# A macaron layer with routed feed-forwards: the rows of the experts' results are gathered tile by tile, and the sums are split alike

## The chip, the core and the metric

The kernel runs on one NeuronCore of a Trainium2 chip. TensorE (PE) multiplies matrices and writes PSUM; VectorE (DVE), ScalarE (ACT) and GpSimd (POOL) work on tiles of 128 partitions in SBUF (VectorE and ScalarE also on PSUM); SyncE (SP) starts most of the transfers. Each engine runs its own list of instructions in order and waits for others at semaphores. Transfers whose addresses come from a tile of indices (gathers) are started by POOL, in POOL's own order, and POOL is occupied while it prepares one.

The metric is the time of one execution on the device, in microseconds. The median of several executions without the profiler is compared; the profile is one more execution, recorded by the hardware.

## The reference

The input is four sequences of 256 tokens with 256 features. The layer is a half feed-forward, an attention, and another half feed-forward with the same weights:

```python
x = x + 0.5 * ffn(layernorm(x), router, w_in, w_out, bias)
x = x + attention(layernorm(x), w_q, w_k, w_v, w_o, b_o)
x = x + 0.5 * ffn(layernorm(x), router, w_in, w_out, bias)

def ffn(x, ...):                      # for each token
    logits = x @ router.T             # 8 experts
    top_vals, top_idx = top_k(logits, 2)
    gates = softmax(top_vals)
    # for each expert e: a, b = split(x @ w_in[e].T); o = (silu(a) * b) @ w_out[e].T
    return sum over the token's two experts of gate * o + bias
```

The hidden width of an expert is 512. The attention has 16 heads of 16 features, is causal, and divides the scores by the square root of 256.

## The kernel before

**Halves and experts.** The 1,024 tokens are worked as two halves, a and b, of four tiles of 128 tokens (two sequences of two tiles). The first feed-forward of the halves is called fa and fb, the second ga and gb. For each of them the tokens are routed (`route_half`): each token gets, for each of its two experts, a place in a table `o_d` in DRAM (`placei`, two indices for each token), and two gates `g`. Then `ffn_half` goes through the eight experts. The rows of an expert's tokens are gathered from DRAM into a tile `xg` (`fetched_rows`, a gather on POOL, three buffers), transposed on TensorE into `pxg` and copied by VectorE to `xT`. `inner(e)` makes four steps, f = 0 to 3, of a product `ph` (L727), the activation on ScalarE (L501) and two steps on VectorE (L502, L503), whose last result is called `hT`. "Step 1.2" below is expert 1, f = 2. `outer(e)` multiplies by `w_out` (L749) and sends the result to `o_d` (L512).

**The sums.** When a feed-forward is done, `combine` brings the results back to the tokens. It takes two tiles (a sequence) at a time. POOL adds half the bias to each tile (L526) and gathers for each token the rows of its first and second expert from `o_d` into tiles `oj` (L532, four buffers): four gathers for a sequence. Then VectorE adds gate times row to the tile (L542), four operations for a sequence. `combine` is a generator that yields after the gathers and after the sums of each sequence, so two yields for a sequence.

**What goes beside what.** The feed-forward of one half runs beside the attention of the other: fb with the attention of half a, ga with that of half b. `ffn_half` and `attention` are generators too, and the main part decides by calls of `run(generator, n)` how many steps of one are written between steps of the other. The first `LEAD` = 7 steps of the feed-forward come before the attention. The attention of a half begins in `ready()`, which makes the sums of a sequence and normalizes it; it is called for the first sequence at the start and for the second while the scores of the first are made. `project` transposes the normalized rows, has them copied by ScalarE (L311), and makes q, k and v (L809, L833), with ScalarE copying q and k out (L818, L822). `maxima` makes the scores (L862, L871, L880) and their maxima on VectorE (L888), head by head; `contexts` makes the weights and applies them; `finish` normalizes and projects. POOL adds the output bias to a tile (L846) behind the projection.

**What sets the order.** The order in which the program writes its instructions is only a start: a scheduler lays them out on each engine by when it expects their operands. `tc.issue_after(ins)` keeps what is written under it behind `ins` on the same engine. `m.hidden` is the last VectorE step of the feed-forward (L503) written so far, `m.gathered` the last gather of rows for an expert. So before the change the sums on VectorE are kept behind the last feed-forward step written, and the bias additions behind the last gather of `xg`. The gathers into `oj` are not held by anything but their operands: the table in DRAM, the indices, and a free buffer.

Of the kernel before, what the change touches and what calls it, by code (L numbers as in the profile page):

```python
# [12 lines left out]
I32 = mybir.dt.int32  # L13
# [3 lines left out]
ALU = mybir.AluOpType  # L17
AX = mybir.AxisListType

P = 128  # L20
# [5 lines left out]
def kernel(  # L26
# [25 lines left out]
    nc = tc.nc  # L52
# [10 lines left out]
    TPB = S // P  # L63
# [15 lines left out]
    LEAD = 7  # L79
# [19 lines left out]
    m = Pools()  # L99
# [11 lines left out]
    def run(steps, n=None):  # L111
        for _ in range(n) if n is not None else iter(int, 1):
            if next(steps, steps) is steps:
                return

    def bank(shape, name, tag="one", bufs=4):
        return ps.tile(shape, F32, tag=tag, name=name, bufs=bufs)
# [13 lines left out]
    for t in range(NTILE):  # L131
        xt = m.xs.tile([P, D], F32, tag="xa", name=f"x_{t}")
# [151 lines left out]
    def norm(xt, name, to=None):  # L284

        n = len(xt)
        mv = m.small.tile([P, n, 2], F32, tag="mv", name=f"mv_{name}")
        for t in range(n):
            st = m.small.tile([P, 6], F32, tag="st", name=f"st_{name}_{t}")
            nc.vector.bn_stats(st, xt[t])  # L290
            nc.vector.bn_aggr(mv[:, t, :], st)
        rstd = rsqrt(mv[:, :, 1], n, name, to)
        res = []
        for t in range(n):
            if t % TPB == 0:
                xn = m.wk.tile([P, TPB, D], F32, tag="xn", name=f"xn_{name}_{t}")
                res.append(xn)
            m.normed = nc.vector.tensor_scalar(
                xn[:, t % TPB, :], xt[t], mv[:, t, 0:1], rstd[:, t : t + 1], ALU.subtract, ALU.mult
            )  # L300
        return res

    def across(xt, name):

        n = len(xt)
        xT = m.wk.tile([P, NDC, n * P], F32, tag="xnT", name=f"xnT_{name}")
        for c in range(NDC):
            pt = bank([P, n * P], f"pxn_{name}_{c}")
            for t in range(n):
                nc.tensor.transpose(pt[:, ts(t, P)], xt[t][:, ts(c, P)], ident)  # L310
            nc.scalar.copy(xT[:, c, :], pt)  # L311
        return xT
# [201 lines left out]
    def combine(xt, o_d, placei, g, name, wide=False):  # L514

        for b in range(len(xt) // TPB):
            rows = []
            if wide and b == 1:  # L520
                two = [
                    m.wk.tile([P, 2, D], F32, tag="xn", name=f"oj_{name}_{t}") for t in range(TPB)
                ]
            for t in range(b * TPB, (b + 1) * TPB):
                with tc.issue_after(m.gathered.ins):
                    nc.gpsimd.tensor_tensor(xt[t], xt[t], bias_bc, ALU.add)  # L526
                for j in range(2):
                    if wide and b == 1:
                        oj = two[t % TPB][:, j, :]
                    else:  # L530
                        oj = m.wk.tile([P, D], F32, tag="oj", name=f"oj_{name}_{t}_{j}", bufs=4)
                    nc.gpsimd.indirect_dma_start(  # L532
                        out=oj,
                        out_offset=None,
                        in_=o_d,
                        in_offset=bass.IndirectOffsetOnAxis(ap=placei[:, t, j : j + 1], axis=0),
                    )
                    rows.append((t, j, oj))
            yield
            with tc.issue_after(m.hidden.ins):  # L540
                for t, j, oj in rows:
                    nc.vector.scalar_tensor_tensor(  # L542
                        xt[t], oj, g[:, t, j : j + 1], xt[t], ALU.mult, ALU.add
                    )
            yield


    def early_logits(xt, name):
# [251 lines left out]
    def project(xt, xn, b):  # L800

        xnT = across([xn[:, t, :] for t in range(TPB)], f"a{b}")
        qkT = []
        for i, wp in enumerate(wqk_sb):
            dst = m.wk.tile([P, NG, S], F32, tag=("qT", "kT")[i], name=f"qk_{b}_{i}")
            pq = bank([P, NDC, S], f"pq_{b}_{i}")
            for j in range(NDC):
                for c in range(NDC):
                    nc.tensor.matmul(  # L809
                        pq[:, j, :],  # L810
                        lhsT=wp[:, c, ts(j, P)],
                        rhs=xnT[:, c, :],
                        start=(c == 0),
                        stop=(c == NDC - 1),
                    )
            for p in range(2):
                if i == 0:
                    nc.scalar.activation(  # L818
                        dst[:, p::2, :], pq, AF.Copy, scale=own_scaled[:, p : p + 1]
                    )  # L820
                else:
                    nc.scalar.activation(  # L822
                        dst[:, p::2, :],
                        pq,
                        AF.Identity,
                        bias=first_row[:, p : p + 1],
                        scale=own[:, p : p + 1],
                    )
            qkT.append(dst)
        pv = bank([P, TPB, D], f"pv_{b}")  # L830
        for t in range(TPB):
            for c in range(NDC):
                m.step = nc.tensor.matmul(  # L833
                    pv[:, t, :],
                    lhsT=xnT[:, c, ts(t, P)],
                    rhs=wv_sb[:, c, :],
                    start=(c == 0),
                    stop=(c == NDC - 1),
                )
        v = v_pad[b % 2]  # L840
        for t in range(TPB):
            nc.scalar.copy(
                v[:, t, 0 : H * HV].rearrange("p (h d) -> p h d", d=HV)[:, :, 0:HD], pv[:, t, :].rearrange("p (h d) -> p h d", d=HD)
            )
        for t in range(TPB):
            nc.gpsimd.tensor_tensor(xt[t], xt[t], bo_bc, ALU.add)  # L846
        return *qkT, v
# [173 lines left out]
    def attention(x1, b0, x2, sums, behind):  # L1021

        n = len(x1) // TPB
        xn = []

        def ready():

            i = len(xn)
            if i < n:
                run(sums, 2)
                xn.extend(norm(x1[i * TPB : (i + 1) * TPB], f"a{b0 + i}"))

        ready()
        yield 4
        last = None
        for i in range(n + 1):
            b = b0 + i  # L1040
            scores = iter(())
            if i < n:
                xt = x1[i * TPB : (i + 1) * TPB]
                qT, kT, v = project(xt, xn[i], b)
                yield 1
                scores = maxima(qT, kT, b)
            if last is None:
                for g, _ in enumerate(scores):
                    if g == 1:
                        ready()  # L1050
                    yield 1
            else:
                ctxT = m.wk.tile([P, NG, S], F32, tag="ctxT", name=f"ctxT_{b - 1}", bufs=1)
                for g, _ in enumerate(contexts(*last[0], ctxT)):
                    more = next(scores, 0) is None
                    if g == 1:
                        ready()
                    yield 2 if more and g % 2 == 0 else 1
                for k, _ in enumerate(finish(ctxT, last[1], b - 1, x2)):
                    yield 1 if i < n else 1 - k  # L1060
                if i < n:
                    run(behind, 1)
            last = (qT, kT, v, b), xt
# [139 lines left out]
    ffn = ffn_half(fa, o_d["fa"], "fa")  # L1203
# [4 lines left out]
    with tc.issue_after(m.sourced.ins):  # L1208


        placei = const.tile([P, 1], I32, name="in_quadi")
# [19 lines left out]
    run(ffn)  # L1231
    ffn = ffn_half(fb, o_d["fb"], "fb")
    sums = combine(xa, o_d["fa"], *fa[2:4], "fa")
    run(sums, 1)
    run(ffn, LEAD)
    ya = []
    route = route_half(ya, 2, "ga", ga)
    run(beside(attention(xa, 0, ya, sums, route), ffn))
# [1 line left out]
    run(ffn)  # L1240
    ffn = ffn_half(ga, o_d["ga"], "ga")
    sums = combine(xb, o_d["fb"], *fb[2:4], "fb")
    run(sums, 1)
    run(ffn, LEAD)
    yb = []
    route = route_half(yb, 3, "gb", gb, True)
    run(beside(attention(xb, BPH, yb, sums, route), ffn))
# [2 lines left out]
    ysum = [bank([P, TPB, D], f"ysum_{i}") for i in range(BPH)]  # L1250
    ffn = ffn_half(gb, o_d["gb"], "gb", gb[5], ysum)
    sums = combine(ya, o_d["ga"], *ga[2:4], "ga")
    run(sums, 1)
    for b in range(BPH):
        run(ffn, LEAD)
        run(sums, 1)
        store(ya[b * TPB : (b + 1) * TPB], b * TPB)
        run(sums, 1)

    run(ffn, 5 * LATE[0] + 5 - BPH * LEAD)  # L1260
    sums = combine(yb, o_d["gb"], *gb[2:4], "gb", True)
    run(sums, 1)
    run(ffn, 9)
    run(sums)
    run(ffn)
    for t in range(TPH):
# [9 lines left out]
    n = nc.values_load(  # L1276
        topi[0:1, 0:1],
        min_val=0,
        max_val=HALF,
        skip_runtime_bounds_check_because="a count of at most the tokens of a half",  # L1280
    )
# [71 lines left out]
```

## Time and profile before

| | us |
|---|---|
| median of 3 runs | 407.78 |
| lowest and highest | 404.29, 407.96 |
| the profiled execution | 427.48 |
| its span, first to last instruction | 425.7 |

In the profiled execution TensorE is busy for 389.7 us, VectorE for 220.3, POOL for 117.3 and ScalarE for 105.2. The mean clock granted to TensorE is 0.956 of full speed. There are 8 gathers into `oj` for each of fa, fb, ga and gb, and 10 into `xg` for each (9 in fa). The chain of work that ended last is empty on this page, so the order of time on the engines has to be read instead.

In a line of the timeline the first number is the start from the beginning of the span, the second the length, both in us; then engine, line of the kernel, operation, what it writes and reads, and how many instructions were merged into the line. In brackets is the idle time before it and who ended it. Matmuls are pipelined and their ends are modelled. For a gather the line shows only the time in which POOL prepares it; when its rows have landed is in the trace's landing records. In a table of stretches each engine has its busy time with the number of its instructions, and the last three columns are TensorE's granted clock, the share of the DMA engines' time, and GB/s.

### The profile page before, as it was taken

The numbers are of one execution on the slowest core, as the hardware profiler recorded it, in microseconds if no ns is written. First come the engines' busy times: TensorE is split into PE (matmuls) and PEld (weight loads), VectorE is DVE, ScalarE is ACT, GpSimd is POOL, SyncE is SP. The second block draws the span as 40 slices with busy tenths as digits, with TensorE's granted clock in tenths as the row PEclk, the third lists the DMA queues.
The fourth block names the chain that finished last, engine by engine and source line by source line (L and its number), as shares of the span: only waits on it lengthen the run. The fifth ranks groups of instructions, "written<-read, shape, count | busy, mean of one in ns | idle before, by whom it ended". The sixth has DMA issues, their size and how long they took to land.

```text
span 425.7 us, 7754 instructions
## 1 busy us (share of the span) xinstructions
PE 389.7 (92%) x2890; PEld 316.0 (74%) x2890; DVE 220.3 (52%) x857; ACT 105.2 (25%) x291; POOL 117.3 (28%) x193
## 2 busy tenths in 40 slices
PE   7699999978989999999986989999999998979993
PEld 4589879766777777778785768767778867878972
DVE  5679434353671256546647294135574863563441
ACT  3122122212205222442111401323163211212210
POOL 5152220453020231230275120133041037540420
PEclk9899999998979699999999997799999999999998
DMA  7989921231000000010233000000000123320211
GB/s 264 343 280 383 371 72 34 69 92 50 13 14 0 14 14 6 21 39 2 79 103 90 15 25 2 1 27 2 26 26 12 39 74 95 104 76 26 62 52 56
DMA packets 16430, 32.71 MB, mean 77 GB/s; under 512 B 2592, under 2 KB 11552, under 8 KB 15360
## 3 DMA queue, kind: packets, MB, share of 16 engines
q1 hardware_dynamic: 12400, 22.30, 14.4%
q0 software_dynamic: 3408, 9.31, 8.0%
q8 instruction: 25, 0.41, 0.4%
q10 hardware_dynamic: 576, 0.52, 0.4%
q14 instruction: 21, 0.17, 0.1%
HBM read 24.26 MB, written 7.86 MB: 75 GB/s over the span
## 4 chain that ended last, share of the span: by engine, by line


## 5 line engine op out<-in xcount | busy, mean ns | idle before, releaser
L888 DVE TENSOR_REDUCE red<-sc 128x3 f32<-128x384 f32 x64 | 31.5, 551 | 58.1 <-PE sc L880 58.1
L941 POOL TENSOR_SCALAR_AFFINE_SELECT pr<-pr 128x256 f32<-128x256 f32 x64 | 24.9, 408 | 98.4 <-ACT pr L939 98.4
L727 PE MATMUL ph_fb<-xT_fb,w_in_sb 128*128 128x160 f32 x256 | 43.8, 320 | 3.4 <-DVE th_fb L502 2.0
L727 PE MATMUL ph_ga<-xT_ga,w_in_sb 128*128 128x160 f32 x256 | 43.8, 320 | 3.0 <-DVE th_ga L502 1.8
L727 PEld LDWEIGHTS ph_fb<-xT_fb,w_in_sb 128*128 128x128 f32 x256 | 39.1, 204 | 5.9 <-DVE th_fb L502 2.4
L727 PEld LDWEIGHTS ph_ga<-xT_ga,w_in_sb 128*128 128x128 f32 x256 | 39.1, 204 | 5.3 <-DVE th_ga L502 2.2
L727 PE MATMUL ph_gb<-xT_gb,w_in_sb 128*128 128x160 f32 x256 | 38.7, 302 | 4.5 <-DVE hT_gb L503 2.3
L727 PEld LDWEIGHTS ph_gb<-xT_gb,w_in_sb 128*128 128x128 f32 x256 | 35.9, 190 | 6.6 <-DVE hT_gb L503 3.3
L727 PE MATMUL ph_fa<-xT_fa,w_in_sb 128*128 128x160 f32 x256 | 38.5, 301 | 0.5 <-ACT xT_fa L784 0.3
L727 PEld LDWEIGHTS ph_fa<-xT_fa,w_in_sb 128*128 128x128 f32 x256 | 36.0, 190 | 1.9 <-DVE hT_fa L503 0.7
L939 ACT ACTIVATE pr<-sT 128x384 f32<-128x384 f32 x64 | 26.2, 496 | 9.1 <-PE sT L929 9.1
L862 PE MATMUL sc<-qk,qk 32*128 32x128 f32 x128 | 24.6, 334 | 3.2 <-DVE red L888 2.3
L862 PEld LDWEIGHTS sc<-qk,qk 32*128 32x128 f32 x128 | 17.0, 190 | 11.5 <-DVE red L888 5.8
L501 ACT ACTIVATE th_fb<-ph_fb 128x160 f32<-128x160 f32 x32 | 9.7, 304 | 61.0 <-PE ph_fb L727 50.5
L502 DVE SCALAR_TENSOR_TENSOR th_gb<-th_gb,ph_gb 128x160 f32<-128x160 f32 x32 | 10.2, 320 | 28.0 <-ACT th_gb L501 23.0
L501 ACT ACTIVATE th_ga<-ph_ga 128x160 f32<-128x160 f32 x32 | 9.7, 304 | 60.2 <-PE ph_ga L727 48.5
L749 PE MATMUL po_ga<-w_out_sb,hT_ga 128*32 128x256 f32 (+1 forms) x128 | 24.3, 399 | 0.0
L871 PE MATMUL sc<-qk,qk 32*128 32x256 f32 x128 | 22.8, 455 | 0.0
L482 POOL DMA_INDIRECT xg_fb<-xn_d_fb,source_fb x10 | 9.5, 953 | 47.5 <-PE pxg_fb L495 34.1
L749 PE MATMUL po_fb<-w_out_sb,hT_fb 128*32 128x256 f32 (+1 forms) x128 | 22.0, 395 | 0.0
L749 PE MATMUL po_gb<-w_out_sb,hT_gb 128*32 128x256 f32 (+1 forms) x128 | 20.6, 382 | 0.5 <-DVE hT_gb L503 0.5
L749 PE MATMUL po_fa<-w_out_sb,hT_fa 128*32 128x256 f32 (+1 forms) x128 | 19.8, 381 | 0.7 <-ACT og_fa L507 0.7
(379 smaller groups left out, 661.2 us busy)
## 6 DMA issues: line engine op xcount, KB each, us to landing
w_in_sb<-in_w_in SPq DMA_DIRECT2D x8, 1024.0 KB
w_out_sb<-in_w_out SPq DMA_DIRECT2D x8, 512.0 KB
o_d_fa<-og_fa SPq DMA_DIRECT2D x10, 128.0 KB
o_d_fb<-og_fb SPq DMA_DIRECT2D x10, 128.0 KB
o_d_ga<-og_ga SPq DMA_DIRECT2D x10, 128.0 KB
out<-y SPq DMA_DIRECT2D x8, 128.0 KB
o_d_gb<-og_gb SPq DMA_DIRECT2D x6, 128.0 KB
x<-in_x ACTq DMA_DIRECT2D x4, 128.0 KB
```

Of the source, the lines that this page charges most:

```text
L482: m.gathered = nc.gpsimd.indirect_dma_start(out=xg, out_offset=None, in_=xn_d, in_offset=bass.IndirectOffsetOnAxis(ap=source[:, i : i + 1] ...
L501: m.bent = nc.scalar.activation(th, ph[0], AF.Tanh, scale=0.5)
L502: nc.vector.scalar_tensor_tensor(th, th, 1.0, ph[0], ALU.add, ALU.mult)
L727: m.inner = nc.tensor.matmul(ph[:, j, :], lhsT=w_in_sb[:, e, c, j * F + f * P : j * F + (f + 1) * P], rhs=xT[e // EG][:, c, e % EG, :], st ...
L749: nc.tensor.matmul(po[r : r + n, :], lhsT=hT[e][:, f, at : at + n], rhs=w_out_sb[:, e, f, :], start=(f == 0), stop=(f == NFC - 1), skip_gr ...
L862: nc.tensor.matmul(s[:, 0, :], lhsT=head(qT, h, slice(0, P)), rhs=head(kT, h, slice(0, P)), start=True, stop=False, skip_group_check=True,)
L871: nc.tensor.matmul(s[:, 1:3, :].rearrange("p a k -> p (a k)"), lhsT=head(qT, h, slice(P, 2 * P)), rhs=head(kT, h, slice(0, 2 * P)), start= ...
L888: nc.vector.tensor_reduce(red[:, h, :], s, AX.X, ALU.max, negate=True)
L939: nc.scalar.activation(pr, s, AF.Exp)
L941: nc.gpsimd.affine_select(out=diag, in_=diag, pattern=[[0, 2], [1, P]], compare_op=ALU.is_ge, fill=0.0, base=0, channel_multiplier=-1,)
```

## The change

`combine` yields after each tile and no longer after each sequence. The two gathers of a tile take their indices from a small tile `at` of their own, which VectorE copies from `placei` behind the last feed-forward step written so far; so the gathers can't start before that step. The sums are split in the same way, two operations (one tile) at a time. The last use of `combine`, for gb (`wide`), makes no copies, and its gathers are written at the same places as before.

The main part spreads the calls: the gathers of the first tile are written after two feed-forward steps, those of the second after four, and the sums of the first tile after seven; those of the second tile are made in the attention's `ready()`. For the second sequence, the gathers of one tile are written behind the projection of the first sequence, those of the other at the first group of scores, the sums of one tile at the second group, and those of the other at the third with the normalization. For the sums of ga, which run beside the feed-forward gb alone, gathers and sums are placed after 1, 3, 6 and 7 steps for the first sequence, and after 2, 4, 6 and 7 further steps for the second.

```diff
         for b in range(len(xt) // TPB):
...
             for t in range(b * TPB, (b + 1) * TPB):
+                at = placei[:, t, :]
+                if not wide:
+                    at = m.small.tile([P, 2], I32, tag="at", name=f"at_{name}_{t}", bufs=4)
+                    with tc.issue_after(m.hidden.ins):
+                        nc.vector.tensor_copy(at, placei[:, t, :])
                 with tc.issue_after(m.gathered.ins):
                     nc.gpsimd.tensor_tensor(xt[t], xt[t], bias_bc, ALU.add)
...
-                        in_offset=bass.IndirectOffsetOnAxis(ap=placei[:, t, j : j + 1], axis=0),
+                        in_offset=bass.IndirectOffsetOnAxis(ap=at[:, j : j + 1], axis=0),
                     )
                     rows.append((t, j, oj))
-            yield
-            with tc.issue_after(m.hidden.ins):
-                for t, j, oj in rows:
-                    nc.vector.scalar_tensor_tensor(
-                        xt[t], oj, g[:, t, j : j + 1], xt[t], ALU.mult, ALU.add
-                    )
-            yield
+                yield
+            while rows:
+                with tc.issue_after(m.hidden.ins):
+                    for t, j, oj in rows[:2]:
+                        nc.vector.scalar_tensor_tensor(
+                            xt[t], oj, g[:, t, j : j + 1], xt[t], ALU.mult, ALU.add
+                        )
+                del rows[:2]
+                yield
...
         def ready():
 
             i = len(xn)
             if i < n:
-                run(sums, 2)
+                run(sums, 1)
...
                 qT, kT, v = project(xt, xn[i], b)
+                run(sums, 1)
                 yield 1
                 scores = maxima(qT, kT, b)
             if last is None:
                 for g, _ in enumerate(scores):
-                    if g == 1:
+                    if g < 2:
+                        run(sums, 1)
+                    if g == 2:
                         ready()
                     yield 1
...
-    run(sums, 1)
-    run(ffn, LEAD)
+    for n in (2, 2, LEAD - 4):
+        run(ffn, n)
+        run(sums, 1)
...
     sums = combine(ya, o_d["ga"], *ga[2:4], "ga")
-    run(sums, 1)
     for b in range(BPH):
-        run(ffn, LEAD)
-        run(sums, 1)
+        for n in (2, 2, 2, 1) if b else (1, 2, 3, 1):
+            run(ffn, n)
+            run(sums, 1)
         store(ya[b * TPB : (b + 1) * TPB], b * TPB)
-        run(sums, 1)
...
     sums = combine(yb, o_d["gb"], *gb[2:4], "gb", True)
-    run(sums, 1)
+    run(sums, TPB)
```

The edit `for n in (2, 2, LEAD - 4)` is made twice, for the sums of fa and of fb. In the order in which the changed program is laid out, TensorE's list is the same but for a place where four products of scores change places, ScalarE's and SyncE's lists are the same, and VectorE's and POOL's differ as said. Lines 526, 532, 542, 727, 846 and 888 of the kernel before are lines 532, 538, 549, 735, 854 and 896 after.

More of the change, by code (lines that the diff above doesn't have):

```diff
@@ L1242 @@
     sums = combine(xb, o_d["fb"], *fb[2:4], "fb")
-    run(sums, 1)
-    run(ffn, LEAD)
+    for n in (2, 2, LEAD - 4):
+        run(ffn, n)
+        run(sums, 1)
     yb = []
@@ L1252 @@
     sums = combine(ya, o_d["ga"], *ga[2:4], "ga")
-    run(sums, 1)
     for b in range(BPH):
-        run(ffn, LEAD)
-        run(sums, 1)
+        for n in (2, 2, 2, 1) if b else (1, 2, 3, 1):
+            run(ffn, n)
+            run(sums, 1)
         store(ya[b * TPB : (b + 1) * TPB], b * TPB)
-        run(sums, 1)
     run(ffn, 5 * LATE[0] + 5 - BPH * LEAD)
     sums = combine(yb, o_d["gb"], *gb[2:4], "gb", True)
-    run(sums, 1)
+    run(sums, TPB)
     run(ffn, 9)
```

## The prediction

> **What bounds the kernel now.** I read the page's busy table and slices first, then the order of time on POOL, TensorE and ScalarE around the places where the sums are made, and last the stretches with the granted clock.
>
> ```profile
> PE 389.7 (92%) x2890; PEld 316.0 (74%) x2890; DVE 220.3 (52%) x857; ACT 105.2 (25%) x291; POOL 117.3 (28%) x193
> PE   7699999978989999999986989999999998979993
> PEclk9899999998979699999999997799999999999998
> ```
>
> TensorE is busy for 92% of the span; nothing else is above 52%. So only two things can move the end: the few places where TensorE stands still, and its clock. The 8th to 10th, 21st and 22nd and 34th to 36th slices have digits below 9. The first two groups are the starts of the fb and ga feed-forwards, where the sums of the half before are made for the attention; the third is the same in gb. In order of time, TensorE in fb:
>
> ```profile
> 86.36 2.34 PE L727 MATMUL ph_fb<-xT_fb,w_in_sb 128*128 128x160 f32 x16
> 88.54 0.59 PE L749 MATMUL po_fb<-w_out_sb,hT_fb 128*128 128x256 f32 x2
> 91.18 1.35 PE L727 MATMUL ph_fb<-xT_fb,w_in_sb 128*128 128x160 f32 x8 [2.04 <-DVE th_fb L502]
> ...
> 95.89 2.44 PE L727 MATMUL ph_fb<-xT_fb,w_in_sb 128*128 128x160 f32 x16 [1.19 <-DVE mv_a L291]
> 99.07 0.76 PE L310 MATMUL pxn_a<-ident,xn_a 128*128 128x128 f32 x4 [0.73 <-DVE xn_a L298]
> 100.98 1.13 PE L809 MATMUL pq<-xnT_a,wq_sb 128*128 128x256 f32 x2 [1.15 <-ACT xnT_a L311]
> ```
>
> Idle: 2.04 + 1.19 + 0.73 + 1.15 = 5.1 us. The same places in ga read 1.83, 1.18, 0.74 and 1.02 = 4.8 us; gb has 2.03 at 359.9 and 1.97 at 374.1. And POOL in the same stretch:
>
> ```profile
> 84.03 0.95 POOL L532 DMA_INDIRECT oj_fa<-o_d_fa,placei_fa  x1 [0.30 <-issue]
> 85.28 0.95 POOL L532 DMA_INDIRECT oj_fa<-o_d_fa,placei_fa  x1 [0.30 <-issue]
> 86.53 0.95 POOL L532 DMA_INDIRECT oj_fa<-o_d_fa,placei_fa  x1 [0.30 <-issue]
> 87.78 0.95 POOL L532 DMA_INDIRECT oj_fa<-o_d_fa,placei_fa  x1 [0.30 <-issue]
> 89.03 0.95 POOL L482 DMA_INDIRECT xg_fb<-xn_d_fb,source_fb  x1 [0.30 <-issue]
> 93.27 0.94 POOL L532 DMA_INDIRECT oj_fa<-o_d_fa,placei_fa  x1 [3.29 <-DVE x L542]
> ```
>
> A gather costs POOL 1.25 us of its queue. Its rows land 2.4 to 2.8 us after it starts (the landing records: the one of 87.78 at 90.14 to 90.22, that of 89.03 at 91.52 to 91.77). What releases TensorE at 91.18 is odd:
>
> ```profile
> 90.11 0.30 ACT L501 ACTIVATE th_fb<-ph_fb 128x160 f32<-128x160 f32 x1 [3.67 <-PE ph_fb L727]
> ```
>
> The product it reads is issued to its end at 87.61, and in nearly all other steps the activation follows 0.04 us later. Here it is 2.5 us late, and the next one 2.9. ga and gb show the same step late by 2.3 and 2.5 us, and there are later cases of 2.0 (fb, 98.33 to 100.36), 1.3 (ga) and 1.1 and 1.5 us (gb). All fall behind four or more gathers that leave POOL one after the other. The 1.15 us before L809 is of this kind too: the transposes end at 99.83, the copies of them start at 100.56.
>
> The profiled execution took 427.48 us (span 425.7, 1.8 around it), 19.7 us above the median of 407.78. Part of this is clock:
>
> ```profile
> 97.70:101.10 3.40, 1.52 (x10) 0.92 (x9) 1.93 (x9) 0.74 (x3) 2.62 (x4) 1.00 0.33 96
> 101.10:104.50 3.40, 3.40 (x9) 2.68 (x10) 0.27 (x1) 0.10 (x1) 0.00 (x0) 0.50 0.00 0
> 118.20:121.60 3.40, 2.18 (x14) 1.32 (x14) 3.26 (x12) 0.30 (x1) 1.91 (x3) 1.00 0.13 39
> 121.60:125.00 3.40, 3.40 (x18) 2.42 (x15) 2.22 (x7) 0.00 (x0) 0.42 (x1) 0.50 0.00 0
> ```
>
> The second column is TensorE's busy time, the third from the end the clock. One stretch of 3.4 us at half speed does 1.7 us of work, so it costs 1.7. There are nine such between the first 20 us and the tail (101.1, and pairs from 121.6, 138.7, 254.7 and 271.8): 15 us. These 15 us and the late activations' idle time (2.0 + 1.8 + 2.0, and 0.7 + 0.6 of the L809 waits) are 22 us, so the unprofiled runs can't have had all of both. I therefore work out each edit with and without late activations.
>
> **The change, part by part.**
>
> *Index copies.* 12 copies of 128x2 on VectorE; the nearest row is the 128x2 cast at L269, 0.17 to 0.22 us. 12 x 0.2 = 2.4 us on an engine that is 48% idle. Those in front of the second pair stand in the norm's chain of 128x2 steps (0.2 us apart, each waiting for the one before), where one more fits between. On the path: 0, at most 4 x 0.2. The Trainium skill (SBUF — State Buffer, the warning on SWDGE) says that a VectorE copy within SBUF can keep GpSimd from writing descriptors until its end and some 0.1 us more. By it each copy costs the gather behind it up to 0.3 us; by the row (L532 takes 942 to 948 ns whatever VectorE does) nothing. I take the row: POOL is not the path.
>
> *First pair of tiles, fb and ga.* The built order puts POOL as xg_3, two adds, xg_9, oj of tile 0 twice, xg_4, oj of tile 1 twice. The slots stay those from 82.78 to 89.03; only xg_4 goes from the last slot to the middle. Its transpose source comes free at 84.85, so it doesn't hold the queue. Tile 1's second gather moves from the slot of 87.78 to that of 89.03, landing 91.77 and not 90.22. The sums (0.40 each, order on VectorE unchanged) start at 92.52: cost 0. Without the late activations they'd be reached at 89.75 (product end 88.70, activation 0.34, two VectorE steps 0.71); the fourth then starts at 91.77 and not 91.0: +0.8 each. Behind it queue the batch norm, th and hT of the third step (TensorE's next step waits for it), and the norm that L310 waits for, so all of it is on the path. Bounds 0 and +0.8.
>
> *Second pair, fb and ga.* The four gathers that left from 93.27 to 97.97, as soon as buffers were free, are now held by copies behind hT of steps 2.1 (98.3) and 2.2, and the latter two stand behind the two L846 adds (1.4 us). So they go at about 98.4, 99.7, 102.1, 103.4 and land by 106. Their sums are due at 112.5: cover 6 us. xg_5 moves ahead of them and waits for a transpose at 93.6; its user comes at 150. POOL's adds are wanted only by the attention's last step. What it may gain: with the run of gathers gone from 93 to 98, the copies at L311 start with the transposes' ends and L809 at 100.25 and not 100.98: -0.7 (ga -0.6). Bounds 0 and -0.7. What it may cost: the gathers now lie beside the projection, where pq goes through ScalarE back to TensorE. The nearest row, handoffs behind two gathers (83.64 and 84.73), was 0.04 late; I take 0, and keep 2 us for each half and handoff.
>
> *The sums beside the scores.* VectorE now makes the reductions 8 to 11 without the two 0.37 us normalizations between them; TensorE waited 0.76 and 0.41 us there (119.63, 121.28). The second wait goes, and 0.15 more: -0.55 each in fb and ga; bounds -0.75 and 0. The normalized tile comes 2 us later than 120.7 and is wanted at 129.
>
> *gb.* First pair: same slots, the sums spread over three steps of equal VectorE work: 0. Second pair: copies behind 1.3 and 2.1, gathers at 365.7, 366.9, 368.3, 369.6, last landing 372.1; sums at 372.36: 0. Without late activations the sums come up to 2 us earlier and wait: +0.7, since TensorE has a step in hand. The last half's own sums (oj_gb) keep their order: 0.
>
> Sum with late activations: -0.7 - 0.6 - 1.1 = -2.4, so 425.1 profiled and 405.4 by the median. Without: 2 x 0.8 + 0.7 - 1.1 = +1.2: 409.0.
>
> **Clock.** The Trainium skill (TensorE: Matmul & The Clock Gate, Part 1) has the clock halved after an idle window of 3.4 us. By it no wait here costs any clock: none is over 2.04 us. The rows say otherwise: windows only 45% and 64% busy (1.52, 2.18 of 3.40) preceded the half clock, though 46% at 224 and at 374 did not. So a shift of 0.5 us can add or save a stretch (1.7) or pair (3.4). I put none into the sum, both into the range.
>
> **Rivals.**
>
> *Forecast: no change, +1.2 us, 409.0* (45%). For: the median is 20 us under the profile that shows the late activations, so the real runs likely have few.
>
> *Spread gathers help, 402.0* (22%). The -2.4, plus the stretch at 101.1 (1.7) and one at 121.6 (1.7) stay at full clock: -5.8. For: both windows lie directly behind the idle time that shrinks. Against: the first run, which costs most (2.0 per half), is still six gathers long, so the change doesn't spread what it seems to.
>
> *Gathers beside the projection delay its handoffs: slower, 415.2* (28%). Place: L311 to L818 and L822, 99 to 107 and 232 to 240. Price: one late handoff of 2.0 per half, and one half-clock stretch of 1.7 behind it: 2 x 3.7 = +7.4. It decides once the handoffs come over 1.2 us late per half, since then the 0.7 and 0.55 are used up. For: TensorE has no other work there, so every late handoff is idle time. Against: no more than two gathers in a row.
>
> The other 5% lies past these. Low end: 402.5, the helped case almost whole; high end 416.5, the slower case and one more stretch. Faster than 1% (under 403.7; 1% is about what a measurement of this kernel can tell from no change, the three runs differ by 0.9%) 0.22; within 1% 0.44; slower 0.34, the rival and the forecast's tail with both waits at their upper bound and a stretch of clock.
>
> **What would show it.** After: the oj gathers of tiles 2 and 3 at L538 between 98 and 105 and between 231 and 238. Right if the activations of L311 and L818 follow TensorE within 0.1 us there, and the L809 wait shrinks from 1.15 to about 0.4; if the sums at L549 never wait for landing by more than 0.8 us; if reductions 8 to 11 run back to back. Wrong if L818 or L822 come 1 us or more behind pq, if VectorE stands before a sum, or if half-clock stretches come or go: then the clock, not the order, made the time.

## The result and the profile after

The changed kernel takes 408.11 us (median of 20 runs, 405.45 to 412.38), the kernel before 405.65 in the same comparison (20 runs, 402.24 to 415.09). The ratio is 1.0081, with a 95% interval of 1.0057 to 1.0105: 0.8% slower, some 3.3 us. The forecast of 409.0 held within a microsecond, but partly because the base came out 2 us lower than the 407.78 it started from: the forecast's own step was +1.2 us, and the measured one is +3.3. Ratios here and below leave out runs over 1.5% above the fastest of their kernel (here 5 of the 20 of before and 1 of the changed kernel's), medians don't, so the two can differ; the means of all runs are 406.98 and 408.23 us, only 1.3 apart.

The profiled execution of the changed kernel took 406.24 us (span 404.5), that of before, in the prediction, 427.48. A third profile of the kernel before, without late activations, is therefore laid beside the changed kernel's below (run `e_before_q`, 410.33 us). Its mean granted clock is 0.967 and the changed kernel's 0.986, so only gaps are compared with it and not times.

The page of the changed kernel: busy time, then TensorE and its clock in 40 slices.

```profile
PE 374.2 (93%) x2890; PEld 305.8 (76%) x2890; DVE 222.8 (55%) x869; ACT 105.6 (26%) x291; POOL 117.8 (29%) x193
PE   6699989997989999999997999999999999989993
PEclk9899999999999999999999999899999999999997
```

TensorE is busy 15.5 us less than in the first profile of before, but this is mostly clock (0.956 there): the nine stretches at half speed that the prediction counted took 15 us, and here one is left between the first 30 us and the tail, in the 26th slice. What the change did has to be read at the places named in the prediction. TensorE in order of time, changed kernel, some of the lines with idle time in front:

```profile
94.21 2.44 PE L735 MATMUL ph_fb<-xT_fb,w_in_sb 128*128 128x160 f32 x16 [1.65 <-DVE hT_fb L503]
97.41 0.76 PE L310 MATMUL pxn_a<-ident,xn_a 128*128 128x128 f32 x4 [0.76 <-DVE xn_a L298]
98.53 1.99 PE L817 MATMUL pq<-xnT_a,wq_sb 128*128 128x256 f32 x8 [0.35 <-ACT xnT_a L311]
...
218.29 2.44 PE L735 MATMUL ph_ga<-xT_ga,w_in_sb 128*128 128x160 f32 x16 [1.62 <-DVE hT_ga L503]
...
330.48 1.25 PE L757 MATMUL po_ga<-w_out_sb,hT_ga 128*128 128x256 f32 x4 [0.75 <-DVE hT_ga L503]
355.31 2.44 PE L735 MATMUL ph_gb<-xT_gb,w_in_sb 128*128 128x160 f32 x16 [1.75 <-DVE hT_gb L503]
```

The 2.04 and 1.19 us of the first profile of before have become one gap of 1.65, and all of these gaps but the 0.35 before the projection are ended by VectorE. In the third profile of before the same view reads:

```profile
93.84 2.44 PE L727 MATMUL ph_fb<-xT_fb,w_in_sb 128*128 128x160 f32 x16 [0.65 <-DVE hT_fb L503]
97.01 0.76 PE L310 MATMUL pxn_a<-ident,xn_a 128*128 128x128 f32 x4 [0.73 <-DVE xn_a L298]
98.12 1.99 PE L809 MATMUL pq<-xnT_a,wq_sb 128*128 128x256 f32 x8 [0.35 <-ACT xnT_a L311]
...
116.74 0.37 PE L862 MATMUL sc<-qk,qk 32*128 32x128 f32 x1 [0.41 <-DVE red L888]
```

So with activations in time the change makes the gap behind the first pair's sums 1.0 us longer in fb (and 0.98 in ga, 0.64 to 1.62), and takes away one gap of 0.41 between the maxima of the scores in each half. (A gap of 0.27 before the maxima's transposes is new. Still, from the start of the line behind the sums to the projection of the next sequence fb takes 28.70 us before, 93.84 to 122.54, and 28.32 after, 94.21 to 122.53.) The wait before the first product of the projection is 0.35 in both. The two places with ga's results, 330.48 and 355.31, were not in the sum at this size. VectorE in the changed kernel in front of the first gap, the sums of fa:

```profile
89.84 0.48 DVE L549 SCALAR_TENSOR_TENSOR x<-oj_fa,g_fa,x 128x256 f32<-128x256 f32 x1
90.79 0.88 DVE L549 SCALAR_TENSOR_TENSOR x<-oj_fa,g_fa,x 128x256 f32<-128x256 f32 x2 [0.47 <-DMA oj_fa<-o_d_fa,at_fa]
92.03 0.48 DVE L549 SCALAR_TENSOR_TENSOR x<-oj_fa,g_fa,x 128x256 f32<-128x256 f32 x1 [0.36 <-DMA oj_fa<-o_d_fa,at_fa]
```

VectorE waits twice for rows to land, 0.47 + 0.36 = 0.83 us (0.44 + 0.36 = 0.80 in ga). In the third profile of before the four sums of this place are one line without a wait:

```profile
90.47 1.67 DVE L542 SCALAR_TENSOR_TENSOR x<-oj_fa,g_fa,x 128x256 f32<-128x256 f32 x4
```

### The profile page after: what moved, and what is told of

Same layout as the page of the kernel before. It is cut to its first block, busy times and chain, and to the rows that moved or that the text cites. A ratio compares the mean times of both kernels' runs of the same rounds, so it can differ in the third digit from the quotient of the medians.

```text
span 404.5 us, 7766 instructions
## 1 busy us (share of the span) xinstructions
PE 374.2 (93%) x2890; PEld 305.8 (76%) x2890; DVE 222.8 (55%) x869; ACT 105.6 (26%) x291; POOL 117.8 (29%) x193
## 4 chain that ended last, share of the span: by engine, by line
## 5 line engine op out<-in xcount | busy, mean ns | idle before, releaser
L735 PE MATMUL ph_ga<-xT_ga,w_in_sb 128*128 128x160 f32 x256 | 41.5, 308 | 1.6 <-DVE hT_ga L503 1.6
L735 PE MATMUL ph_fb<-xT_fb,w_in_sb 128*128 128x160 f32 x256 | 40.5, 303 | 1.8 <-DVE hT_fb L503 1.6
L735 PEld LDWEIGHTS ph_ga<-xT_ga,w_in_sb 128*128 128x128 f32 x256 | 37.1, 195 | 3.5 <-DVE hT_ga L503 2.2
L735 PEld LDWEIGHTS ph_fb<-xT_fb,w_in_sb 128*128 128x128 f32 x256 | 36.0, 190 | 3.9 <-DVE hT_fb L503 2.2
L870 PE MATMUL sc<-qk,qk 32*128 32x128 f32 x128 | 23.3, 321 | 2.3 <-DVE red L896 1.5
L757 PE MATMUL po_fb<-w_out_sb,hT_fb 128*32 128x256 f32 (+1 forms) x128 | 20.9, 385 | 0.0
L502 DVE SCALAR_TENSOR_TENSOR th_fa<-th_fa,ph_fa 128x160 f32<-128x160 f32 x32 | 10.2, 319 | 17.7 <-ACT th_fa L501 17.5
```

The lines of the kernel that those rows point to most:

```text
L502: nc.vector.scalar_tensor_tensor(th, th, 1.0, ph[0], ALU.add, ALU.mult)
L735: m.inner = nc.tensor.matmul(ph[:, j, :], lhsT=w_in_sb[:, e, c, j * F + f * P : j * F + (f + 1) * P], rhs=xT[e // EG][:, c, e % EG, :], st ...
L757: nc.tensor.matmul(po[r : r + n, :], lhsT=hT[e][:, f, at : at + n], rhs=w_out_sb[:, e, f, :], start=(f == 0), stop=(f == NFC - 1), skip_gr ...
L870: nc.tensor.matmul(s[:, 0, :], lhsT=head(qT, h, slice(0, P)), rhs=head(kT, h, slice(0, P)), start=True, stop=False, skip_group_check=True,)
```

## The experiments

Twelve runs were made in three groups, each on another chip (chips 6, 3 and 1). On the first the kernel before takes 423.44 us (median of 43 runs), on the second and third 405.59 (70 runs) and 405.55 (59). Which chip the comparison at the top and the first profile of before ran on is not known. Each ratio is to the kernel before in the same group; runs of different groups are compared by their ratios.

### Before, a second profile

No edit.

> The kernel before, unchanged, for a second profile to lay beside that of the changed kernel. If the late activations are a thing of the first profile alone, ScalarE follows the products in fb and ga within 0.1 us here, VectorE reaches the first pair's sums about 1.1 us after the product and waits for no landing, and TensorE's gap before the first product behind the sums is about 0.8 us shorter than the 1.65 and 1.62 us of the changed kernel, and in gb about 0.7 shorter than 1.75. If the late activations belong to the gathers themselves, gaps of 2 us stand at the same places as in the first profile.

Measured: 420.57 us (one run). The activations come late here too. ScalarE in fb, order of time:

```profile
86.42 0.30 ACT L501 ACTIVATE th_fb<-ph_fb 128x160 f32<-128x160 f32 x1 [1.07 <-DVE hT_fb L503]
90.32 0.30 ACT L501 ACTIVATE th_fb<-ph_fb 128x160 f32<-128x160 f32 x1 [3.60 <-PE ph_fb L727]
91.80 0.30 ACT L501 ACTIVATE th_fb<-ph_fb 128x160 f32<-128x160 f32 x1 [1.17 <-remote]
```

The product read at 90.32 has its end at 87.9, so the activation is 2.4 us late, as in the first profile. All four profiles of this group show such steps in fb, ga and gb. The first case of the expectation fell: late activations are not a thing of one execution.

### The first sequence alone

The two-tile copies, gathers and sums of fa and fb for the first sequence; `combine` keeps the old form for the second, and the attention is that of before. Of the edit, the main part (it stands twice):

```diff
-    run(sums, 1)
-    run(ffn, LEAD)
+    for n in (2, 2, LEAD - 4):
+        run(ffn, n)
+        run(sums, 1)
```

> Only the first sequence of fa and fb is changed (two-tile copies, tile-by-tile gathers and sums); the second sequence and ga as before. Theory 'late fourth gather': tile 1's second gather stands behind a gather for an expert and lands 1.25 us later, VectorE waits 0.8 us in fb and in ga with TensorE idle behind it: +1.6 us against before (1.004). Rival 'the second sequence's gathers and sums make the loss': 0 (1.000). Rival 'clock': no fixed sum, the granted clock differs from that of before by over 0.003.

Measured: 425.66 us median, ratio 0.9947 (0.9899 to 0.9994). The median is 2.2 us above that of before and the ratio below 1, so the times of this group, which spread widely, can't tell 1.6 us of loss from none. VectorE in fb shows why none need be expected:

```profile
94.48 1.67 DVE L549 SCALAR_TENSOR_TENSOR x<-oj_fa,g_fa,x 128x256 f32<-128x256 f32 x4
```

The fourth gather leaves POOL at 90.50, one slot late, but the sums are only reached at 94.48, behind a late activation, and wait for nothing. This is the cover that the prediction named for the case with late activations.

### The second sequence alone

The copies, gathers and sums of fa and fb for the second sequence, and the attention's calls; the first sequence as before. Of the edit, two of the attention's calls:

```diff
                 qT, kT, v = project(xt, xn[i], b)
+                run(sums, 1)
...
-                    if g == 1:
+                    if g < 2:
+                        run(sums, 1)
+                    if g == 2:
                         ready()
```

> Only the second sequence of fa and fb is changed (gathers beside the projection, sums at the second and third group of scores); the first sequence and ga as before. Theory 'late fourth gather': nothing of the loss is here, the smaller gap between the maxima of the scores gives -0.8 to -1.1 us (0.997 to 0.998). Rival 'second sequence': the gathers and copies beside the projection and norm cost what the changed kernel lost, +1.5 to +3 us (1.004 to 1.008).

Measured: 414.07 us median (6 runs, 412.64 to 416.11, all under the lowest of before, 417.33), ratio 0.9846 (0.9791 to 0.9901), a gain of some 6.5 us. On this chip it is larger than anything in the sum. ScalarE in its profile:

```profile
100.26 0.30 ACT L501 ACTIVATE th_fb<-ph_fb 128x160 f32<-128x160 f32 x1 [1.83 <-PE ph_fb L734]
```

This activation, of step 2.2, follows its product, where the one of before was 1.5 us late behind five gathers in a row (run `e_before`, 100.59). The gathers now leave at 99.56, 100.81, 103.35 and 104.62, and ScalarE's steps of the projection stand beside them with waits for TensorE alone.

### ga's sums alone

```diff
-    run(sums, 1)
     for b in range(BPH):
-        run(ffn, LEAD)
-        run(sums, 1)
+        for n in (2, 2, 2, 1) if b else (1, 2, 3, 1):
+            run(ffn, n)
+            run(sums, 1)
         store(ya[b * TPB : (b + 1) * TPB], b * TPB)
-        run(sums, 1)
```

> Only the sums of ga, beside the feed-forward gb, are changed. Theory: the last gathers of its second sequence leave POOL behind two gathers for experts and land at the time of the sums, VectorE waits 0.7 us: +0.7 us (1.002). Rival 'no cost, TensorE has a step in hand': 0. Rival 'most of the loss is here': +2 us or more (1.005).

Measured: 422.71 us median, ratio 0.9978 (0.9934 to 1.0022). It can't be told from no change on this chip.

### The changed kernel once more

No edit, on the second chip. The profiles of this and of all later runs show no late activations in fb, ga and gb.

> The changed kernel once more, beside its parts. Theory 'landing and late activations': what it is worth depends on whether activations come late behind runs of gathers. Where they don't (ScalarE within 0.1 us of the products), VectorE's waits for landing decide: +2.5 to +3.5 us against before (1.006 to 1.009). Where they do, the waits are covered and the gathers spread beside the projection gain: -3 to -7 us (0.983 to 0.993). Rival 'the change is worth the same everywhere': +3.3 us (1.008) either way.

Measured: 408.51 us median, ratio 1.0099 (1.0068 to 1.0129), which repeats the result. Its profile has something that the first one lacks. VectorE at the sums of fa:

```profile
89.20 0.48 DVE L549 SCALAR_TENSOR_TENSOR x<-oj_fa,g_fa,x 128x256 f32<-128x256 f32 x1
90.12 0.88 DVE L549 SCALAR_TENSOR_TENSOR x<-oj_fa,g_fa,x 128x256 f32<-128x256 f32 x2 [0.44 <-DMA oj_fa<-o_d_fa,at_fa]
93.48 0.48 DVE L549 SCALAR_TENSOR_TENSOR x<-oj_fa,g_fa,x 128x256 f32<-128x256 f32 x1 [2.47 <-DMA oj_fa<-o_d_fa,at_fa]
```

The fourth sum waits 2.47 us and not 0.36, and TensorE's gap behind it is 3.74 us:

```profile
95.66 0.54 PE L735 MATMUL ph_fb<-xT_fb,w_in_sb 128*128 128x160 f32 x2 [3.74 <-DVE hT_fb L503]
```

In ga of this execution VectorE's four sums wait for nothing (218.49, 1.67 us) and TensorE's gap behind them is 0.65, as before the change: TensorE had stood shortly before, 0.65, 0.83 and 1.18 us, for rows of the first experts, and the sums came later. So what the late gather costs differs from place to place and from execution to execution.

The landing records of fa's fourth gather have sixteen parts: fifteen landed by 91.36, 2.8 us after its start, the last at 93.39, 4.8 after it. In that stretch (90.5 to 92.5) the DMA queues of this run read:

```profile
q1 hardware_dynamic: 138, 0.13, 19.6%
q0 software_dynamic: 39, 0.09, 12.4%
q8 instruction: 1, 0.02, 2.8%
```

The one packet of the queue "instruction" is a code load of 16 KB that starts at 91.28. Nine profiles, the changed kernel's first and all of the second and third group, have the landing records nearly whole. They hold 531 gathers after 70 us, and 24 of these have a last part that landed over 0.6 us behind the fifteenth. In the flight of each of the 24 there is a code load of 8 or 16 KB. In the flight of 186 others there is one too, and no part is late; without a code load in flight none of 321 is late. So a late part goes with a code load, but a code load holds a part only now and then. In fb a load of 16 KB comes once near this place, between 91 and 94 us, in every one of the nine. In the third profile of before the gathers in flight at that time have rows of an expert or of the second sequence, which are wanted later; in the changed kernel it can be the fourth gather of the sums. In its first profile it was, too (load at 91.36, gather started at 89.24), and the last part recorded landed at 91.93, in time. After the gap of 3.74, a stretch of half clock follows (the stretches of this run; the third number from the end is the clock):

```profile
88.80:95.90 7.10, 3.36 (x23) 2.97 (x22) 4.15 (x17) 0.98 (x3) 1.67 (x2) 1.00 0.25 76
96.10:99.50 3.40, 3.40 (x16) 3.29 (x15) 2.62 (x15) 0.30 (x1) 0.52 (x1) 0.54 0.00 0
```

### Tile 1's gathers back in front

```diff
-    for n in (2, 2, LEAD - 4):
+    for n in (2, 1, LEAD - 3):
```

With this copy one step earlier the built order of POOL is again four gathers of the sums and then the one of the fifth expert.

> The changed kernel with tile 1's index copy held one feed-forward step earlier, so that its two gathers leave POOL ahead of the fifth expert's gather, as before the change. Theory 'late fourth gather': the first pair's rows land 1.25 us earlier, VectorE waits no more, -0.8 us each in fb and ga against the changed kernel (-1.6, 0.996 of it), where activations come in time; 0 where they come late. Rival 'second sequence or copies': no gain over the changed kernel.

Measured: 404.82 us median, ratio 1.0005 (0.998 to 1.0031), against 1.0099 for the changed kernel: 3.8 us less. VectorE and TensorE of this run in fb, at the same place:

```profile
91.39 1.67 DVE L549 SCALAR_TENSOR_TENSOR x<-oj_fa,g_fa,x 128x256 f32<-128x256 f32 x4
```

```profile
94.75 1.49 PE L735 MATMUL ph_fb<-xT_fb,w_in_sb 128*128 128x160 f32 x9 [0.64 <-DVE hT_fb L503]
```

Both waits are gone, here and in ga (0.64). The order of one gather is thus the largest part of the loss: this the edit shows. How the 3.8 us are made up is argued from single profiles: idle time of 2 x 1.0 = 2.0 us in the changed kernel's first profile, and 3.1 in its second, at fb's sums, where the late part met them, with none at ga's. The mean granted clock of the runs rises too, from 0.980 to 0.986. In this run the late part falls on the expert's gather (landing 4.8 us after its start), and nobody waits for it. The theory held; the size expected, 1.6, was too small.

### The same, with ga's sums as before

The edit of the run before it, and for ga the old `combine` (no copies, four sums at a time) and the old main part. Of the edit, the main part:

```diff
-    for b in range(BPH):
-        for n in (2, 2, 2, 1) if b else (1, 2, 3, 1):
-            run(ffn, n)
-            run(sums, 1)
-        store(ya[b * TPB : (b + 1) * TPB], b * TPB)
+    run(sums, 1)
+    for b in range(BPH):
+        run(ffn, LEAD)
+        run(sums, 1)
+        store(ya[b * TPB : (b + 1) * TPB], b * TPB)
+        run(sums, 1)
```

> As the run with tile 1's copy held earlier, and ga's sums as before the change. Theory: where activations come in time, a further -0.7 us against that run, and -0.8 to -1.1 us against before (0.997 to 0.998), since only the gain between the maxima of the scores is left; where they come late, like the kernel with only the second sequence changed (0.985). Rival 'holding the gathers costs by itself': +1 us or more against before.

Measured: 401.74 us median, ratio 0.9931 (0.9905 to 0.9957). This beats both kernels: 2.8 us under before. ga's part therefore costs 0.0074, 3.0 us, where 0.7 was expected. Neither the gap of 0.75 before ga's last product nor the one of 1.75 in gb is in its trace.

### The second sequence alone, once more

The kernel of the third run, on the second chip.

> Only the second sequence of fa and fb changed, once more, beside the changed kernel. Theory: -0.8 to -1.1 us against before (0.997 to 0.998) where activations come in time, -4 to -8 us (0.980 to 0.990) where they come late. Rival 'second sequence loses': above 1.002 where they come in time.

Measured: 402.32 us median, ratio 0.9939 (0.9914 to 0.9963), a gain of 2.5 us. The rival, that the second sequence loses, is out on both chips. What the ratio doesn't show is the spread: of the 70 runs of before in this group 18 lie over 408 us, up to 413.79, and of these 22 none lies over 404.61. Why is not shown.

### Before, a third profile

No edit.

> The kernel before, for a profile beside those of the parts. Where activations come in time: the sums of the first pair wait for no landing in fb and ga (four sums in 1.7 us), the gap behind them on TensorE is about 0.65 us as in the run with tile 1's copy held earlier, the last product of ga shows no 0.74 us gap, and gb has no 1.74 us gap. What the second sequence's change saves must then show as gaps of before between 94 and 102 us and between the maxima of the scores: 0.8 to 1.3 us for each half.

Measured: 410.33 us (one run). It ran on the third chip. Its lines are shown at the result: no wait for landing, a gap of 0.65, and 0.41 between the maxima. The gap in gb was not nought as expected: 1.45 us. There the sums were in time but one of them took 2.23 us beside two additions of POOL, so this place costs something in some executions of the kernel before as well.

### ga's bias additions early

As the run with tile 1's gathers in front, and:

```diff
-        for n in (2, 2, 2, 1) if b else (1, 2, 3, 1):
+        for n in (2, 2, 2, 1) if b else (0, 0, 6, 1):
```

> As the run with tile 1's copy held earlier (1.0005 of before), but the first sequence of ga's sums has its bias additions and copies written ahead of gb's first step, as before the change. Theory 'POOL's additions slow VectorE': the two additions no longer lie beside VectorE's spread matrices (0.54 us alone, 0.95 beside them), the gap of 0.74 us before ga's last product goes: -0.7 us, 0.9987 of before. Rival 'only the late landing in gb costs': 1.0005.

Measured: 403.54 us median, ratio 0.9986 (0.9967 to 1.0005), 0.8 us less than without the edit (1.0005, in the second group), with intervals that overlap. The times alone don't decide between the expectation and its rival; the traces show what the edit does. VectorE at the end of ga, changed kernel, where POOL makes its first two additions for ga from 327.33 to 328.99:

```profile
327.47 2.72 DVE L678 TENSOR_SCALAR spread<-lanes,prod_gbrows 128x512 f32<-128x512 f32 x4
330.11 0.31 DVE L503 TENSOR_TENSOR hT_ga<-th_ga,ph_ga 128x160 f32<-128x160 f32 x1
```

and in this run, where POOL is idle at that time:

```profile
325.41 1.91 DVE L678 TENSOR_SCALAR spread<-lanes,prod_gbrows 128x512 f32<-128x512 f32 x4
327.23 0.32 DVE L503 TENSOR_TENSOR hT_ga<-th_ga,ph_ga 128x160 f32<-128x160 f32 x1
```

Four matrices of 512 columns take 0.54 us each alone and up to 0.95 beside the additions; the last step of ga, for which TensorE's last product waits, comes 0.8 us later. The gap before that product is gone in this run.

The Trainium skill (SBUF — State Buffer, "Who interferes with whom") says that VectorE and GpSimd share one pair of ports, that a `tensor_scalar` of VectorE can need the shared pair, and that who starts first then holds it for the whole instruction. The rows fit that: a matrix is held for up to 0.41 us (0.95 - 0.54), less than the 0.73 us of one addition, and the two additions take 1.66 us instead of 1.41. That the ports are the cause no run here shows by itself. By that rule the price of moving an addition is read from what VectorE does at its new place, which the prediction did not look at.

### ga's second sequence early

As the run with tile 1's gathers in front, and:

```diff
-        for n in (2, 2, 2, 1) if b else (1, 2, 3, 1):
+        for n in (0, 0, 6, 1) if b else (1, 2, 3, 1):
```

> As the run with tile 1's copy held earlier (1.0005 of before), but the copies of ga's second sequence are written at the start of their seven steps, so that its four gathers leave POOL ahead of the sixth expert's. Theory 'late landing in gb': the sums of the second sequence no longer wait 0.7 us, and the gap of 1.74 us behind them falls to under 0.7: -1.1 to -1.8 us, 0.9961 to 0.9978 of before. Rival 'TensorE has a step in hand': 1.0005.

Measured: 403.90 us median, ratio 0.9987 (0.9964 to 1.001), 0.7 us less than without the edit (1.0005, in the second group), intervals overlapping, and less than the 1.1 to 1.8 expected. VectorE in gb, changed kernel:

```profile
350.40 0.48 DVE L549 SCALAR_TENSOR_TENSOR y<-oj_ga,g_ga,y 128x256 f32<-128x256 f32 x1
351.61 2.73 DVE L549 SCALAR_TENSOR_TENSOR y<-oj_ga,g_ga,y 128x256 f32<-128x256 f32 x3 [0.73 <-DMA oj_ga<-o_d_ga,at_ga]
```

The second sum waits 0.73 us for its rows, and then three sums take 2.73 us instead of 1.3, because by now POOL is at the additions for the next sequences:

```profile
351.23 0.94 POOL L482 DMA_INDIRECT xg_gb<-xn_d_gb,source_gb  x1 [0.34 <-PE pxg_gb L495]
352.18 1.88 POOL L532 TENSOR_TENSOR y<-y,bias_bc 128x256 f32<-128x256 f32 x2
```

In the run with early gathers the four sums read:

```profile
348.36 2.18 DVE L549 SCALAR_TENSOR_TENSOR y<-oj_ga,g_ga,y 128x256 f32<-128x256 f32 x4
```

No wait, and only the end of the sums meets the additions: 2.18 us from first to last instead of 3.94. TensorE's gap of 1.75 is gone. Of the 1.76 us that the sums save, 0.73 are the wait for landing and 1.0 is time beside the additions: the wait had brought a second delay, larger than itself.

### Both

> Both edits of the two runs before it: bias additions of ga's first sequence early, gathers of its second sequence early; sums and yields still tile by tile. Theory: the two add up, -1.8 to -2.5 us, 0.9943 to 0.9960 of before, near the kernel that leaves ga's sums as they were (0.9931). Rival 'the copies or the split sums cost by themselves': stays 1 us or more above that kernel.

The edit is `for n in (0, 0, 6, 1)` for both sequences.

Measured: 402.20 us median, ratio 0.994 (0.9916 to 0.9964), 2.6 us less than with tile 1's gathers in front alone. The kernel that leaves ga as it was (0.9931, in the second group) lies within this interval. So the two causes make up most of ga's part, 2.6 of 3.0 us: a cost of the copies and the split sums themselves isn't seen, and with intervals of 1 us to either side a small one isn't excluded. The sum of the two alone, 1.5 us, is less than 2.6, within the width of the intervals.

## Why the prediction was right, and where it was not

**The ground: with or without late activations.** The forecast worked each edit out both ways and took the case without. The changed kernel's profile and all of the second and third group show none in fb, ga and gb, so that was the right branch. Its reason, that the median lies 20 us under the profile with late activations, holds as far as it goes. But they are not a chance of single executions: on the chip of the first group all profiles have them and the kernel before takes some 18 us more. The 427.48 us of the first profile lie inside that group's range of before (417.33 to 432.47) and above all 149 other runs of before (up to 415.87), so it may have come from the same chip. Late activations go with the chip or with something that goes with it.

**The signs it named.** Two came out for it: in the changed kernel's profile ScalarE follows TensorE in the projection, with a wait of 0.35, and reductions 8 to 11 run back to back. Two came out against it: VectorE stands before the sums, 0.83, 0.80 and 0.73 us in the first profile, and a sum waits 2.47 in the second.

**Index copies, 0.** Held: in the run with both of ga's edits all copies are there, and it is, within its interval, as fast as the kernel without ga's. The gathers into `oj` still take 0.94 to 0.97 us of POOL, so no copy is seen to hold them up, and the row that the prediction took held.

**First pair, +0.8 in fb and in ga.** The mechanism held step by step: tile 1's second gather in the last slot, VectorE waiting 0.83 and 0.80 us, and TensorE behind it. The term was mis-sized. TensorE loses 1.0 and 0.98, and undoing it is worth 3.8 us in the runs, not 1.6. One cause that the profiles show is a part of the gather that lands 2 us behind the others, with a code load in flight; behind that gap the clock fell, in the one profile that has it. How often this happens in the runs is not known. The upper bound of +0.8 was drawn from landings of 2.4 to 2.8 us, of which the records of that profile are thin: of the sixteen parts of the gather of 87.78 they hold three. A bound from the landing of one gather leaves out what may hold back a single part.

**Second pair, gathers beside the projection.** New place 0: held. The gathers of tiles 2 and 3 left POOL at 97.03 to 102.09 and ScalarE's steps followed TensorE. The gain of 0.7 at the projection belongs to late activations; without them the wait is 0.35 before and after. The rival "gathers beside the projection delay its handoffs" is wrong on both chips: the second sequence alone gains, 0.9939 and 0.9846.

**Sums beside the scores, -0.55 each.** One gap of 0.41 went in each half, so 0.14 too much was taken. Yet the runs give 2.5 us for the whole second sequence, and 0.8 is all that these gaps explain. The mean granted clock of the runs that the ratio counts is higher by 0.002 (by itself some 0.7 us); the rest lies inside the interval or is not explained.

**gb, 0 for the first pair and +0.7 for the second.** The second pair's wait is 0.73, as said (one sum of the first pair waits too, 0.26). The step that failed is "First pair: same slots, the sums spread over three steps of equal VectorE work: 0". It costed the gathers and the sums, and left out the two bias additions that are written with them. Held behind a later gather, they came to lie beside VectorE's spread matrices, and TensorE stood 0.75 us. In the second pair the wait pushed the sums under POOL's next additions, and three of them took 1.4 us longer. TensorE's two gaps, 0.75 and 1.75, are 2.5 of the 3.0 us of ga's part.

**The sum.** Foreseen without late activations: 2 x 0.8 + 0.7 - 1.1 = +1.2. Measured by undoing parts: 3.8 + 3.0 - 2.8 = +4.0, where the 2.8 is what is left when both losses are undone, so that the three make up the 1.0099 of that group by construction; in the comparison at the top it was +3.3. So the sign was right and the places of loss and gain too, but both losses were too small by more than half, and so was the gain. That the sum came out within 2 or 3 us is luck: the errors have opposite signs. The rival "spread gathers help" would have been the better text for the first chip: there the second sequence alone gains 1.5%, but the whole change was not run there.

## What to carry to other kernels

When a gather is moved by one slot in its queue, ask who needs its last part, and leave room for a part that comes 2 us late (here 4.8 us after the start and not 2.8): a gather whose rows are wanted at once should stand in front of one whose rows are wanted later. When a group of instructions is moved, cost each of them, also the small one on the other engine: here two additions on POOL of 0.7 us held TensorE for 0.75, and no cost of the twelve new copies is seen. A wait of 0.7 us is not worth 0.7 us if what follows it runs into something else.

## What the runs showed of the hardware

- **Late activations came on one chip of three.** The same kernel before shows ScalarE 2.4 us behind TensorE under five or six gathers in a row on one chip (420.57 us) and nowhere in fb, ga and gb on another (410.33 us), with the same run of gathers in front of fb's sums. What holds ScalarE there wasn't found.
- **Late parts of gathers go with code loads.** Of 210 gathers with a code load of 8 or 16 KB in flight 24 have a last part over 0.6 us behind the other fifteen, up to 2.1 us (2.71 and 4.83 us after the start, with tile 1's gathers in front); of 321 without one none has. Those gathers cost nothing when their rows are wanted later.
- **VectorE beside POOL's additions.** A sum of 0.48 us takes 0.94 to 1.04 and a matrix of 0.54 us up to 0.95 while POOL adds two tiles, and the additions take 0.9 to 1.0 instead of 0.73. In the third profile of before one sum beside two additions took 2.23 us, and the additions their usual 0.73.
